# One ring of three tiles for the experts' relu results and the statistics' loads

## The chip, the cores and the metric

The kernel runs on one core of a Trainium2 chip. The metric is the device time of one execution in microseconds (us); the median of several runs is given. A profile of one execution shows what each engine did: TensorE (PE; PEld is its weight load), VectorE (DVE), ScalarE (ACT), GpSimd (POOL) and SyncE (SP), which here issues nearly all DMAs.

## The reference, cut to what matters

Two layers on images of 8 x 384 channels x 32 x 32 in float32. The first is a selective state space scan with a group norm before it and an MLP behind it, the second a mixture of four experts of which each token weighs two.

```python
def reference(x, ...):
    # layer 0: group norm, layer norm, in_proj, conv, silu, scan over 1024 tokens with 16 states,
    #          gate, out_proj, MLP with gelu
    x = x + _L0_conv_ref(_gn(x), ...)
    # layer 1: group norm, gate softmax, top 2, and for each expert e:
    #   hdn = relu(x @ w1[e] + b1[e]);  y = hdn @ w2[e] + b2[e];  out = sum_e coef[e] * y
    x = x + _L1_conv_ref(_gn(x), ...)
    return x
```

The group norm takes a mean and a variance over 12 channels and all tokens of an image. So the statistics of an image must be complete before its first product.

## The kernel before

The 8 images are cut into 16 chunks of 512 tokens (`NCH`), two to an image; a chunk's activations are three tiles of 128 channels x 512 tokens. The scan has 24 rounds for each chunk, 384 in all (`scan_chains`). A round has four exponentials on ScalarE (the decays, line 842), four scans on DVE (line 862), a drive product on POOL (line 854), a read-out on DVE and one on POOL (line 866), and a sum over states on TensorE (line 888). Everything else fills the room beside the rounds: the input projection of the next chunk (`in_proj`, line 328), the output projection of the last one (line 539), the MLP (`hidden`, line 561; `second`, line 603), and the first products of the experts (line 714), which come last in rank.

The order of instructions on all engines is fixed while the program is built. A planner keeps a clock of its own for each engine; costs such as `MM`, `ACT`, `DVE` and `DMA` (3.5 us) are written at the top of the file. Every piece of work is a task, a Python generator that yields the engine it wants next and the time it will take; `yield "-", us` means to wait so long, `yield "bank", us` to wait for one of four PSUM banks as well. `issue_one` picks for each engine a late task, else the next step of a round, else a task that fits. What the planner thinks of time thus decides only the order; on the chip each engine runs through its list and waits on semaphores.

Two kinds of work use the tiles that the change touches.

The statistics of the next image (`statistics`, begun in the third round of an even chunk) read the image once more, in six pieces of 128 x 512 (256 KB). Each piece is loaded by SP into the tile `part` (line 264), and DVE takes its sums (`bn_stats`, line 267). There is one such tile, in the pool `pst`. The first image is read from the tiles of its chunks instead.

The experts' first products come in units (`expert_lane`): 12 for each chunk, 192 in all, each of three products with weights from a stream of three buffers (`e_w`, loaded by SP, line 240). A unit's PSUM bank is emptied by `expert_evict`: ScalarE writes the relu into a tile `r` (line 728), and SP writes that to DRAM (line 731). There are two such tiles, in the pool `pr`. A list `writing` holds the units on their way, and a third one has to wait, with its bank, until one has left the list, 3.5 us of the planner's clock after its write-out was given out. On the chip the relu waits until the write-out of the tile's last content has really landed.

The first half of the units of chunk 13 and all before it can be placed beside the scans; the others come behind them (lines 708 and 709). After the scans `second_layers` reads the relu results back and forms the experts' second products (line 1210), 1152 matmul records in a row.

Of the kernel before, what the change touches and what calls it, by code (L numbers as in the profile page):

```python
# [11 lines left out]
F32 = mybir.dt.float32  # L12
# [6 lines left out]
P = 128  # L19
B, C, L = 8, 384, 1024  # L20
T = 512
# [4 lines left out]
ND = DI // P  # L26
NS = 16
Q = 4
NG = NS // Q
TOP = 16.0  # L30
HID = 9
# [16 lines left out]
POLL = 0.5  # L48
# [9 lines left out]
def chunk_of(dram, i):  # L58

    b, h = divmod(i, NH)  # L60
    return dram[b].rearrange("(p j) (n s) w -> n p j (s w)", p=P, n=NH)[h]
# [6 lines left out]
def build(tc, io):  # L68
# [3 lines left out]
    with ExitStack() as outer:  # L72
# [47 lines left out]
        with ExitStack() as ctx:  # L120
            layers(ctx, tc, io, ident, cmean, eps, dram, x1_dram, gn1, logits, r_dram, group_norm)


def layers(ctx, tc, io, ident, cmean, eps, dram, x1_dram, gn1, logits, r_dram, group_norm):
# [9 lines left out]
    def pool(name, bufs, stack=ctx, **kw):  # L134
        return stack.enter_context(tc.tile_pool(name=name, bufs=bufs, **kw))


    wp, p2, px1, pxn = pool("wp", 1), pool("p2", 2), pool("px1", 2), pool("pxn", 1)
    psq, pr, pw_e = pool("psq", 2), pool("pr", 2), pool("pw_e", 3)
    ps_g = pool("ps_g", BANKS, space=PSUM)  # L140
    scanning = ctx.enter_context(ExitStack())
    p1, pdt, pxt, pdu = (pool(name, bufs, scanning)
                         for name, bufs in (("p1", 1), ("pdt", 2), ("pxt", NH), ("pdu", 3)))
    pz, pxc, ph, pbc, pst = (pool(name, bufs, scanning)
                             for name, bufs in (("pz", ND), ("pxc", 2 * ND), ("ph", HID), ("pbc", NG), ("pst", 1)))
    pw_in, pw_out, pw_1, pw_2 = (pool("pw_" + name, 3, scanning) for name in ("in", "out", "1", "2"))
    ps_a, ps_b, ps_y = (pool("ps_" + name, 1, scanning, space=PSUM) for name in "aby")

# [69 lines left out]
    def bank(name):  # L218
        held[0] += 1
        current[0].holds += 1  # L220
        return ps_g.tile([P, T], F32, name=name, tag="g")

    def free():
        held[0] -= 1
        current[0].holds -= 1
# [26 lines left out]

    def statistics(b):
        st = p2.tile([P, NH * J, 6], F32, name="st")
        for k in range(NH):
            for j in range(J):
                if b == 0:
                    part = xt[k][:, j, :]  # L260
                else:
                    yield "-", 8
                    part = pst.tile([P, T], F32, name="part")
                    nc.sync.dma_start(part, chunk_of(io["x"], b * NH + k)[:, j, :])
                    yield "-", 2 * DMA
                yield "DVE", DVE
                V.bn_stats(st[:, k * J + j, :], part)
        g = wp.tile([P, 2], F32, name=f"gn{b}")
        yield from group_norm(st, bank, free, p2, g)

        yield "bank", 0.25
        small = bank("shift")
        PE.matmul(small[:, 0:1], lhsT=cmean, rhs=g[:, 1:2], start=True, stop=True)
        yield "ACT", 0.65
        mean_w = p1.tile([P, P], F32, name="mean_w")
        S.activation(mean_w, cmean, AF.Identity, scale=g[:, 0:1])
        S.activation(g[:, 1:2], small[:, 0:1], AF.Identity, bias=g[:, 1:2], scale=-float(J))
        yield "-", 0
        free()
        gn[b] = g, mean_w  # L280
# [416 lines left out]
    def expert_lane():  # L697

        for i in range(NCH):
            if i < NCH - NH:  # L700
                yield from load_xn(i)
            while i not in scored:
                yield "-", POLL

            xn = xns.pop(i) if i < NCH - NH else x1[i]
            for u in range(E * J):

                while i == NCH - NH - 1 and u >= E * J // 2 and summed.get(NCH - 1) != J:
                    yield "-", POLL
                yield "bank", 3 * MM  # L710
                w = streams["e_w1"].take("e_w1", u)
                h = bank("e_hid")
                for j in range(J):
                    PE.matmul(h, lhsT=w[:, j, :], rhs=xn[:, j, :], start=(j == 0), stop=(j == J - 1))  # L714

                current[0].holds -= 1
                begin(expert_evict(h, i, u), rank=1, after=now[0] + 3 * MM, holds=1)
            yield "-", 0

    writing = []  # L720

    def expert_evict(h, i, u):
        while len(writing) == 2:
            yield "-", POLL
        writing.append((i, u))
        yield "ACT", ACT
        r = pr.tile([P, T], F32, name="r")
        S.activation(r, h, AF.Relu, bias=e_b1[:, u:u + 1])
        yield "-", 0
        free()  # L730
        nc.sync.dma_start(r_dram[i][u], r)
        yield "-", DMA
        writing.remove((i, u))


    coef_dram = dram.tile([NT, E, P], F32, name="coef_dram")
# [307 lines left out]
    def plan(i, k):  # L1044

        n = i + 1
        if k % 4 == 1 and k // 4 + 2 < ND:
            begin(delta(i, k // 4 + 2), rank=0)
        if k in (2, 3, 4):
            begin(gate(i, k + 1))  # L1050
        if k == 4:
            begin(silus(zs, gates, [(i, d) for d in range(3, 6)]))
        if n < NCH:
            if 4 <= k < 10:
                begin(conv(n, k - 4), rank=1)
            if k in (6, 9):
                begin(silus(xc, accs, [(n, k - 6 + d) for d in range(3)]), rank=1)
            if k in (11, 12, 13):
                begin(gate(n, k - 11))
            if k == 9:  # L1060
                begin(x_proj(n), rank=1)
            if k == 13:
                begin(silus(zs, gates, [(n, d) for d in range(3)]))
            if k == 15:
                begin(delta(n, 0), rank=0)
            if k == 20:
                begin(delta(n, 1), rank=0)
        if k == 20 and n + 1 < NCH:
            begin(norm(n + 1), rank=1)
        if k == 3 and i + NH < NCH:  # L1070
            begin(next_x(i))
        if k == 3 and i % NH == 0 and i + NH < NCH:
            begin(statistics(i // NH + 1), rank=3)
# [169 lines left out]
    with tc.manual_schedule():  # L1243
        w_in = Stream(pw_in, [("in_proj", k) for k in in_order()])

        begin(statistics(0), idle_products())
        run(everything)
        begin(norm(0))
        run(everything)
        S.preload_act_table_set(SILU_SET)  # L1250
        begin(*(conv(0, d, at_once=True) for d in range(ND)), x_proj(0))
        run(lambda: len(xc) == ND)
        exp_ln_tables()
        run(everything)
        load_b(0, 0)
        load_c(0, 0)
        begin(delta(0, 0))
        run(everything)
        for s in range(1, NG):
            load_b(0, s)  # L1260
            load_c(0, s)
        begin(delta(0, 1), rank=0)
        begin(*(gate(0, d) for d in range(3)))
        begin(silus(zs, gates, [(0, d) for d in range(3)]))
        begin(norm(1))
        seed(0, 0)
        begin(lanes())
        scan_chains()
        run(lambda: summed.get(NCH - 1) == J)
        scanning.close()  # L1270
        second_layers()
# [41 lines left out]
```

## Time and profile before

| | |
|---|---|
| median of 3 runs | 3779.09 us (3776.12 to 3780.9) |
| the profiled execution | 3780.1 us |
| its span, first to last instruction | 3778.4 us |
| mean granted TensorE clock | 0.968 |
| busy: PE, DVE, POOL, ACT | 3586.7, 3027.0, 2771.8, 2377.7 us |
| relus of the experts (line 728) | 192 of 682 ns (median), from 700.0 to 3278.9 us |
| loads for the statistics (line 264) | 42, landing after 4.0 us (median), issued from 103.7 to 2500.8 us |
| second products of the experts (line 1210) | from 3278.6 us to the end |

The span has a beginning of some 650 us in which the pipeline fills, the scans with all fillers to about 3103 us, a stage of what is left over, and from 3279 us the second products of the experts. A matmul of float32 shows as two records in the profile. A busy share is a mean over these stages.

### The profile page before, as it was taken

What the parts mean: (1) busy time and instruction counts of PE and PEld (TensorE: products, weight loads), DVE (VectorE), ACT (ScalarE), POOL (GpSimd) and SP (SyncE); (2) the same over time, 40 slices, a digit from 0 to 9 for tenths busy, and PEclk for the clock granted to TensorE, in tenths of its full rate; (3) what the DMA queues carried; (4) which work ended last, traced back from release to release, by engine and by line L of the source; (5) the groups of instructions that cost most, each with busy time, mean ns of one, the idle gap of its engine ahead of it and who ended that gap; (6) DMA issues with size and microseconds to landing.
All of it is one profiled execution on the core that took longest, in us unless ns stands there. A gap on an engine that the chain in (4) does not pass through costs nothing.

```text
span 3778.4 us, 35513 instructions
## 1 busy us (share of the span) xinstructions
PE 3586.7 (95%) x10342; PEld 1369.7 (36%) x10342; DVE 3027.0 (80%) x3099; ACT 2377.7 (63%) x3714; POOL 2771.8 (73%) x1069
## 2 busy tenths in 40 slices
PE   7769898999999999999999999999999999999999
PEld 3213232333333333333333333333333333444444
DVE  4898999899889888998899898988898870355554
ACT  4657686877786778777877787787777753200000
POOL 2998999999889998999889998998899970000000
PEclk8769898999999999999999999999999999999999
DMA  3434454565656565656555555655555543655553
GB/s 118 143 126 148 153 173 160 180 201 184 200 180 203 183 194 181 211 183 202 187 195 191 183 186 175 208 194 181 183 193 191 192 160 131 227 184 184 184 190 105
DMA packets 387925, 674.78 MB, mean 179 GB/s; under 512 B 42876, under 2 KB 153852, under 8 KB 385556
## 3 DMA queue, kind: packets, MB, share of 16 engines
q1 hardware_dynamic: 385568, 672.18, 53.6%
q8 instruction: 83, 1.36, 0.2%
q14 instruction: 110, 0.90, 0.1%
q10 hardware_dynamic: 2164, 0.34, 0.1%
HBM read 534.33 MB, written 138.02 MB: 178 GB/s over the span
## 4 chain that ended last, share of the span: by engine, by line
PE 60%; DVE 13%; ACT 11%; POOL 7%; issue 4%; DMA 4%; SPq 1%; POOLq 0%; DVEq 0%; ACTq 0%
PE acc L1210 13%; PE e_hid L714 9%; PE acc L603 8%; PE hid L561 7%; PE g_in L328 7%; PE y L888 6%; DVE da_A L862 5%; POOL du L854 5%; PE g_out L539 4%; DVE du L862 4%; ACT da_A L842 3%; DVE du L866 2%; POOL du L866 2%; PE g_dt L455 2%; ACT da_B L842 1%
## 5 line engine op out<-in xcount | busy, mean ns | idle before, releaser
L854 POOL TENSOR_TENSOR du<-dxr,b 128x2048 f32<-128x2048 f32 x383 | 1735.1, 4536 | 62.6 <-PE y L888 46.2
L866 POOL TENSOR_TENSOR du<-du,c 128x1024 f32<-128x1024 f32 x384 | 905.8, 2359 | 137.8 <-DVE du L862 107.3
L842 ACT ACTIVATE da_A<-dtr_a,w_a_log 128x512 f32<-128x512 f32 x768 | 529.4, 689 | 262.9 <-DVE du L866 105.8
L842 ACT ACTIVATE da_B<-dtr_b,w_a_log 128x512 f32<-128x512 f32 x768 | 525.9, 685 | 253.4 <-DVE du L862 240.7
L328 PE MATMUL g_in<-xt,in_proj 128*128 128x512 f32 x1152 | 549.7, 619 | 24.4 <-ACT xt L319 11.3
L862 DVE TENSOR_TENSOR_SCAN du<-da_B,carry,du 128x512 f32<-128x512 f32 x384 | 487.7, 1270 | 90.1 <-ACT da_B L842 81.6
L603 PE MATMUL acc<-h,mlp_w 128*128 128x512 f32 x1152 | 538.6, 607 | 12.3 <-ACT h L577 5.3
L888 PE MATMUL y<-du,sel 128*32 128x512 f32 x3072 | 470.4, 629 | 78.0 <-DVE du L866 40.8
L862 DVE TENSOR_TENSOR_SCAN da_A<-da_A,carry,du 128x512 f32<-128x512 f32 x384 | 491.4, 1280 | 53.5 <-ACT da_A L842 49.2
L561 PE MATMUL hid<-tt,mlp_w 128*128 128x512 f32 x1152 | 522.5, 598 | 9.7 <-ACT sq L675 1.8
L862 DVE TENSOR_TENSOR_SCAN du<-da_B,du 128x512 f32<-128x512 f32 x384 | 464.4, 1209 | 68.6 <-ACT da_B L842 46.2
L862 DVE TENSOR_TENSOR_SCAN da_A<-da_A,du 128x512 f32<-128x512 f32 x384 | 467.6, 1218 | 45.3 <-ACT da_A L842 37.2
L1210 PE MATMUL acc<-r,w_e_w 128*128 128x512 f32 x1152 | 494.6, 592 | 0.0
L714 PE MATMUL e_hid<-xn,e_w 128*128 128x512 f32 x1008 | 470.5, 606 | 24.2 <-DMA e_w<-in_e_w 15.0
L866 DVE TENSOR_TENSOR du<-da_A,c 128x1024 f32<-128x1024 f32 x384 | 467.7, 1218 | 9.0
L328 PEld LDWEIGHTS g_in<-xt,in_proj 128*128 128x128 f32 x1152 | 216.6, 195 | 346.8 <-issue 270.2
L603 PEld LDWEIGHTS acc<-h,mlp_w 128*128 128x128 f32 x1152 | 211.0, 191 | 324.9 <-issue 253.7
L561 PEld LDWEIGHTS hid<-tt,mlp_w 128*128 128x128 f32 x1152 | 213.1, 190 | 302.9 <-issue 249.9
L1210 PEld LDWEIGHTS acc<-r,w_e_w 128*128 128x128 f32 x1152 | 218.9, 190 | 275.5 <-issue 275.5
L714 PEld LDWEIGHTS e_hid<-xn,e_w 128*128 128x128 f32 x1008 | 188.6, 192 | 284.0 <-issue 233.1
L539 PE MATMUL g_out<-xc,out_proj 128*128 128x512 f32 x576 | 268.8, 606 | 1.8 <-DMA out_proj<-in_out_proj 1.8
L888 PEld LDWEIGHTS y<-du,sel 128*32 128x32 f32 x3072 | 71.2, 109 | 412.5 <-issue 110.3
(133 smaller groups left out, 3061.8 us busy)
## 6 DMA issues: line engine op xcount, KB each, us to landing
dxr<-dxr_dram SPq DMA_DIRECT2D x384, 256.0 KB, 4.7
mlp_w<-in_mlp_w SPq DMA_DIRECT2D x384, 192.0 KB, 3.6
dtr_b<-dtr_dram SPq DMA_DIRECT2D x192, 256.0 KB, 4.0
dtr_a<-dtr_dram SPq DMA_DIRECT2D x192, 256.0 KB, 3.2
r_dram<-r SPq DMA_DIRECT2D x192, 256.0 KB, 3.3
r<-r_dram SPq DMA_DIRECT2D x64, 768.0 KB, 4.6
in_proj<-in_in_proj SPq DMA_DIRECT2D x192, 192.0 KB, 3.4
e_w<-in_e_w SPq DMA_DIRECT2D x192, 192.0 KB, 3.9
```

What stands on the lines that cost most here:

```text
L328: PE.matmul(g, lhsT=w[:, j, :], rhs=xt[i][:, j, :], start=(j == 0), stop=(j == J - 1))
L455: PE.matmul(g, lhsT=w_dt[:, d * P:(d + 1) * P], rhs=dbc[i][0:DTR, :], start=True, stop=True)
L539: PE.matmul(g, lhsT=w[:, d, :], rhs=xc[i, 3 * k + d], start=(k + d == 0), stop=(k == 1 and d == 2))
L561: PE.matmul(g, lhsT=w[:, j, :], rhs=tt[i][:, j, :], start=(j == 0), stop=(j == J - 1))
L603: PE.matmul(g, lhsT=w[:, n, :], rhs=hs[mine[n]], start=(k + n == 0), stop=(k == 1 and n == 2))
L714: PE.matmul(h, lhsT=w[:, j, :], rhs=xn[:, j, :], start=(j == 0), stop=(j == J - 1))
L842: S.activation(out, dtr[i, d][pair][:, j % 2, :], AF.Exp, scale=neg_a[:, d, j, s:s + 1])
L854: G.tensor_tensor(du[r], dxr[i, d], wide(bt[i, s].unsqueeze(1), [P, Q, T]), ALU.mult)
L862: V.tensor_tensor_scan(a if j < 2 else b, a, b, start, ALU.mult, ALU.add)
L866: engine.tensor_tensor(du[r][:, js, :], h, wide(ct[i, s].unsqueeze(1), [P, 2, T]), ALU.mult)
L888: PE.matmul(y[j * m:(j + 1) * m, :], lhsT=sel, rhs=h[:, j, :], start=False, stop=(s == NG - 1), tile_position=(0, j * m), skip_group_check ...
L1210: PE.matmul(acc[j], lhsT=e2[:, e, d, j, :], rhs=r[:, d, :], start=(e + d == 0), stop=(e + d == E + J - 2))
```

## The change

The pool `pst` and the list `writing` go. The pool `pr` gives out three tiles once, `r0` to `r2`, and a list `spare` holds those that are free. A task that needs one takes the first of the list, or asks again each 0.5 us of the planner's clock, and appends it at the end of the list when it is done: the experts 3.5 us after the write-out was given out, the statistics as soon as `bn_stats` has been given out. The experts take their tile before they ask for ScalarE, the statistics theirs before the load. So up to three relu results can be on their way while no statistics are loaded, and the room in memory is the same.

```diff
-    psq, pr, pw_e = pool("psq", 2), pool("pr", 2), pool("pw_e", 3)
+    psq, pr, pw_e = pool("psq", 2), pool("pr", 1), pool("pw_e", 3)
...
-    pz, pxc, ph, pbc, pst = (pool(name, bufs, scanning)
-                             for name, bufs in (("pz", ND), ("pxc", 2 * ND), ("ph", HID), ("pbc", NG), ("pst", 1)))
+    pz, pxc, ph, pbc = (pool(name, bufs, scanning)
+                             for name, bufs in (("pz", ND), ("pxc", 2 * ND), ("ph", HID), ("pbc", NG)))
...
+    spare = deque(pr.tile([P, T], F32, name=f"r{k}") for k in range(3))
+
     def statistics(b):
...
                     yield "-", 8
-                    part = pst.tile([P, T], F32, name="part")
+                    while not spare:
+                        yield "-", POLL
+                    part = spare.popleft()
                     nc.sync.dma_start(part, chunk_of(io["x"], b * NH + k)[:, j, :])
                     yield "-", 2 * DMA
                 yield "DVE", DVE
                 V.bn_stats(st[:, k * J + j, :], part)
+                if b > 0:
+                    spare.append(part)
...
-    writing = []
-
     def expert_evict(h, i, u):
-        while len(writing) == 2:
-            yield "-", POLL
-        writing.append((i, u))
+        while not spare:
+            yield "-", POLL
+        r = spare.popleft()
         yield "ACT", ACT
-        r = pr.tile([P, T], F32, name="r")
         S.activation(r, h, AF.Relu, bias=e_b1[:, u:u + 1])
         yield "-", 0
         free()
         nc.sync.dma_start(r_dram[i][u], r)
         yield "-", DMA
-        writing.remove((i, u))
+        spare.append(r)
```

## The prediction

> **What bounds the kernel now.** I read the page's busy shares first, then the busy time by stretches, then the TensorE gaps in the timeline, and last the answer for the tile r, since the change is about when that tile comes free.
>
> ```profile
> PE 3586.7 (95%) x10342; PEld 1369.7 (36%) x10342; DVE 3027.0 (80%) x3099; ACT 2377.7 (63%) x3714; POOL 2771.8 (73%) x1069
> ```
>
> TensorE is busy 95% of the span. The missing 192 us are not spread evenly. The stretches (columns: stretch, length, busy of PE, PEld, DVE, ACT, POOL, clock, DMA share, GB/s):
>
> ```profile
> 189.00:283.00 94.00, 60.92 (x156) 14.75 (x156) 85.70 (x89) 53.18 (x85) 91.04 (x40) 0.66 0.37 126
> 1134.00:1512.00 378.00, 369.28 (x1125) 137.42 (x1123) 339.06 (x341) 292.67 (x457) 347.75 (x133) 0.99 0.58 191
> 1889.00:2267.00 378.00, 366.10 (x1120) 137.34 (x1118) 342.14 (x345) 290.93 (x458) 343.85 (x132) 0.99 0.58 189
> 2645.00:3023.00 378.00, 372.51 (x1143) 139.41 (x1140) 332.34 (x329) 289.22 (x437) 352.07 (x135) 1.00 0.57 190
> 3306.00:3400.00 94.00, 94.00 (x220) 41.61 (x219) 50.07 (x57) 0.00 (x0) 0.00 (x0) 1.00 0.52 184
> ```
>
> Most idle time is in the first 650 us, where POOL is the fuller engine and no expert product exists yet. From 650 us to the last scan (3103 us) TensorE idles only 51 us, adding up its gaps in the timeline, and POOL and DVE run at 89 to 93%. After 3279 us it never stops. A change in the experts' relu tiles can win at most a part of those 51 us, and a few in the stage between 3103 and 3279 us. The tile r:
>
> ```profile
> L728 ACT ACTIVATE r<-e_hid,w_e_b x192: 665/682/694, 700.0 to 3278.9; 128x512 f32<-128x512 f32 x192
>   DMA r_dram<-r: 44.7, 19
> DMA to landing us min/median/max: 2.0/4.3/12.0
> ```
>
> In 19 of 192 cases ScalarE, which works in order, stood before a relu until an earlier write-out of the same tile had landed, 44.7 us together. Six of these (17.0 us) come after 3160 us. The other thirteen (27.7 us) stand in the scans, where decays (line 842) queue behind the relu. One shows the whole damage:
>
> ```profile
> 2145.49 0.69 ACT L728 ACTIVATE r<-e_hid,w_e_b 128x512 f32<-128x512 f32 x1 [3.17 <-DMA r_dram<-r]
> 2146.08 0.68 ACT L842 ACTIVATE da_B<-dtr_b,w_a_log 128x512 f32<-128x512 f32 x1
> ...
> 2147.55 0.38 PE L273 MATMUL shift<-gn,cmean 128*128 128x1 f32 x2 [4.21 <-ACT gn L116]
> ...
> 2149.12 5.49 PE L290 MATMUL mu<-xt,mean_w 128*128 128x512 f32 x6 [1.18 <-ACT mean_w L276]
> ```
>
> The relu waits 3.17 us, the statistics chain behind it is late, TensorE stands 4.21 us, and then six matmuls take 5.49 us in place of 2.74: the clock granted in 2148 to 2156 us is 0.56 to 0.58. The gap itself and the slow matmuls (2.75 us) and sums (1.36 for 1.06) after it are all paid.
>
> **Is TensorE really the bound?** The Trainium skill, Perfetto Trace Analysis, section Identifying the Most-Contended Engine, holds matmul busy time a bad measure and wants the weight loads' share, here 36%. By that rule TensorE has room, gaps on it are free, and the sum below would lose its only positive term: 3775. The trace speaks otherwise: twelve expert units near the end, 72 matmul records back to back, take 31.14 us, 0.43 us each, and nothing else limits them. Float32 products fill TensorE although weights load quickly. I take the row, and charge gaps.
>
> **The change part by part.**
>
> *The same work.* No instruction is added or removed: still 192 relus, 192 write-outs, 42 loads for statistics, 42 bn_stats. Three 128x512 tiles before (two r, one part), three after. What changes is who may have which, and, as the order of all engines is written down by the planner while the program is built, the order. In the changed program TensorE's order is the same up to the 2100th of 5174 instructions (about round 189 of 384, near 1600 us). From there 138 of the 384 rounds stand with a different count of expert products, mostly one or two units ahead, and at the last round both have given out 161 units. The 31 units left over after the scans, and TensorE's and DVE's order from there, are the same.
>
> *Waits on the write-out.* A write-out frees its tile 0.68 + 4.3 = 5.0 us after the relu starts. With two tiles that is one relu per 2.5 us, and a unit takes TensorE 31.14/12 = 2.6 us, so two tiles just carry the median; every late landing (up to 12.0) makes a wait. Here the skill speaks against the change: DMA: Bandwidth & Descriptors, section Anatomy of one DMA, fits 2.0 us fixed plus bytes over 436 GB/s, an estimate of 2.6 us for 256 KB, so (0.68 + 2.6)/2 = 1.6 us per relu. By that rule two tiles were plenty and the third is worth nothing; by the row it is worth the waits. I take the row, as the waits are there. In the changed order no relu of the scans finds its tile written by one of the last 7 ScalarE instructions (before: 10 relus did), and within 10 instructions 3 do (before: 27). So nearly all of the 27.7 us goes from ScalarE. What TensorE gets of it: I take each gap that follows such a wait, at most as long as the wait: 1.24 (1390 us, where the expert's weights landed late in the same moment, so it may stay), 3.17 (2147), 0.59 (2898), 0.74 (2929): 5.7 us, and 3.05 for the slow clock after 2147, 8.8 at most. The other waits, some 22 us, have no TensorE gap near them: cover is TensorE's own queue, which holds some microseconds of ready products; without it they would be won too. Only the 1.24 lies in the part whose order stays; in place of the rest another gap may come. Value: -5, most of the 6.2 at 2147; ends 0 and -8.8.
>
> *Statistics in the ring.* A load holds a tile for the planner's 7 us and the wait for DVE, 36 times while experts run: then the experts have two tiles, as before. A load now also waits, on the SP queue, for the last write-out of its tile. In three cases the two stand only 4, 6 and 7 SP instructions apart; at 0.3 to 0.5 us an issue, the landing of 4.3 us leaves 2.5, 1.5 and 1 us of waiting, with weight loads and the dtr and dxr repeats queued behind. SP stands idle for 250 us for relus alone (its own waits), and what it issues is wanted microseconds later, so I take 0; without that cover 5 us. No relu got a wait on DVE, though a tile is given back when bn_stats is issued: ScalarE has always waited for a later DVE instruction already: 0. The statistics themselves have 17 + 24 rounds of 8 us before they are needed, against six loads of some 20 us: 0.
>
> *The new order from round 189.* Per round POOL needs 4.54 + 2.36 + 1.27/4 = 7.2 us, so a stretch of rounds with less than 7.2 us of TensorE work each leaves it dry, unless it is behind. I put TensorE's work on the rounds (0.86 per 128x512 product, 1.06 per round's sums). Over 8-round stretches, rounds 176 to 384, the shortfall comes to 19.2 us before and 24.6 after; over 4 rounds 40.2 and 44.0; over 3 rounds 57.0 and 58.0. The 8-round figure is near the 25 us that TensorE really idled from 1650 us on, so I weigh it about half: +3; ends 0 and +7. The trace can't show gaps of an order that hasn't run: a newly drawn order of that length could as well have 15 or 40 us of gaps for these 25.
>
> *After the scans.* TensorE stands 2.72 us for h, 6.00 and 1.40 us for e_w. The first e_w is queued on SP behind the stores of x1, the last behind the coefficients, as in the new order. ScalarE's 17.0 us there hold up nobody. In the new order three e_w loads stand behind the write-out of the unit that frees their buffer, 0.77 us later than now: 0 to +2.3, value 0. From 3279 us: 0.
>
> Sum: the profiled execution took 3780.1 us (span 3778.4 and 1.7 around it), 1.0 above the median of 3779.1. 3780.1 - 5 + 3 = 3778.1.
>
> **The rivals.** *Nearly nothing (likeliest), 3778.* The waits go, most are covered, and the order gives back part. For it: the 51 us of gaps in 2450 us, the same tail.
>
> *Faster, 3768.* All 8.8 us come back, the weak stretches cost nothing because TensorE is behind there, and the redrawn part loses a few more gaps of e_w and xn: 3780.1 - 8.8 - 3. For it: a gap of 9 us in all waits for e_w since 650 us. Against: those stand mostly where no relu waited.
>
> *Slower, 3796.* Experts let go earlier leave later rounds without filling. In the new order rounds 213 to 220 are 9.0 us short (before 1.2) and 357 to 364 are 8.4 (before 6.6): 9.6 us more, and if each comes as one stand of over 3 or 4 us, the slow clock adds 3.05 twice: 3780.1 + 9.6 + 6.1 = 3795.8, with no wait won. It decides once the shortfall is larger than the products TensorE still has queued. Against: shortfalls of 6.5 us before (rounds 305 and 357) left no gap over 3 us.
>
> *It doesn't do what it says.* If clumps of four relus came as often as clumps of three, the third tile would change nothing: 3780 with any order. The distances on ScalarE speak against it.
>
> **How the numbers follow.** Likeliest case 0.51, faster 0.22, slower 0.27. About 0.2%, 7.6 us, is what a measurement of this kernel can tell from no change: below 3771.5 counts as faster, above 3786.7 as slower; the likeliest case lies between, with its own range 3772 to 3786. The unknown is the gaps of the new order, 15 to 40 for 25 us, and clock losses after them, so the range goes from 3762 to 3797.
>
> **What would show it.** Waits of r on r_dram before 3103 us should fall from 27.7 us to under 8. TensorE's gaps before 1600 us should be about 1 us fewer. From 1600 to 3103 us they should stay within 15 to 40 us; the places to look are rounds 213 to 220 (about 1760 to 1830 us) and 357 to 364 (2910 to 2970). The stage from 3103 us should keep its length of 675 us within 2. I am wrong if gaps over 3.5 us with a clock of 0.5 after them appear, or if POOL starts to wait for dxr behind a statistics load on SP.

## The result, and the profile after

The changed kernel takes 3792.11 us (median of 9 runs, 3784.2 to 3796.11) where the kernel before takes 3779.09 (9 runs): 1.0029 of it, 95% interval 1.0021 to 1.0038. It is slower by 11 us, 8 to 14. The likeliest forecast was no change.

The page of the changed kernel shows nearly the same sums:

```profile
PE 3584.2 (95%) x10342; PEld 1369.9 (36%) x10342; DVE 3028.1 (80%) x3099; ACT 2379.6 (63%) x3714; POOL 2771.1 (73%) x1069
```

The span is 9.9 us longer, and TensorE is busy 2.5 us less, so some 12 us more of gaps. The stretches (the same columns as before: PE, PEld, DVE, ACT, POOL, clock, DMA share, GB/s):

```profile
1134.00:1512.00 378.00, 370.16 (x1125) 138.61 (x1124) 342.15 (x345) 293.85 (x459) 348.64 (x134) 0.99 0.58 190
1889.00:2267.00 378.00, 364.75 (x1119) 136.56 (x1117) 335.57 (x338) 286.90 (x452) 339.30 (x131) 0.99 0.57 191
2645.00:3023.00 378.00, 373.95 (x1152) 139.67 (x1145) 334.13 (x329) 294.85 (x444) 352.07 (x134) 0.99 0.57 189
3306.00:3400.00 94.00, 94.00 (x220) 41.61 (x219) 52.05 (x59) 0.00 (x0) 0.00 (x0) 1.00 0.55 190
```

From 1889 to 2267 us all engines do less in the same time than before (POOL 339.3 us for 343.9, DVE 335.6 for 342.1). The last stage is unchanged. The tile r answers as follows; the change's own effect is complete:

```profile
L731 ACT ACTIVATE r<-e_hid,w_e_b x192: 664/681/690, 701.5 to 3288.4; 128x512 f32<-128x512 f32 x192
...
L268 SPq DMA_DIRECT2D r<-in_x x42: 327/430/592, 104.6 to 2501.9; - x42
...
  PE e_hid L720: 138.5, 70
```

There is no line for r_dram left. 44.7 us of waits on the write-out are gone. Instead the relus wait for TensorE, 138.5 us in 70 cases where it was 83.8 in 43. This alone is no sign of a loss: a relu that no longer waits for its tile waits for its product instead, and a faster kernel below shows 107.2 us in 51 cases. The loss shows where TensorE stands before its expert products (line 720, 714 before). One such place in the timeline (start, length, engine, instruction, in brackets the idle time before it):

```profile
1982.91 1.07 PE L891 MATMUL y<-du,sel 128*32 128x512 f32 x8
...
1983.53 2.43 SPq L380 DMA_DIRECT2D xn<-xn_dram  x3
...
1989.32 4.58 PE L720 MATMUL e_hid<-xn,e_w 128*128 128x512 f32 x6 [5.34 <-ACT da_B L845]
...
1993.74 2.74 PE L545 MATMUL g_out<-xc,out_proj 128*128 128x512 f32 x6
...
1993.94 0.69 ACT L731 ACTIVATE r<-e_hid,w_e_b 128x512 f32<-128x512 f32 x1 [5.28 <-PE e_hid L720]
```

Between 1982.9 and 1989.3 TensorE has just finished the last unit of a chunk, and its next instruction is the first unit of the next chunk. Both use the one tile xn, so the three pieces of the new chunk can be loaded only now, from 1983.53 on, and a piece lands 5.0 us after its issue (median). The profile names a decay as the releaser, but that decay is no input of this product; I take the loads to have landed last, which the runs without them test below. Then the six matmuls run at half clock at first, 4.58 us in place of 2.74. I call this a switch.

### The profile page after: what moved, and what is told of

Same layout as the page of the kernel before. It is cut to its first block, busy times and chain, and to the rows that moved or that the text cites. A ratio compares the mean times of both kernels' runs of the same rounds, so it can differ in the third digit from the quotient of the medians.

```text
span 3788.3 us, 35527 instructions
## 1 busy us (share of the span) xinstructions
PE 3584.2 (95%) x10342; PEld 1369.9 (36%) x10342; DVE 3028.1 (80%) x3099; ACT 2379.6 (63%) x3714; POOL 2771.1 (73%) x1069
## 4 chain that ended last, share of the span: by engine, by line
PE 62%; DVE 14%; ACT 13%; POOL 4%; DMA 4%; issue 3%; SPq 1%; DVEq 0%; POOLq 0%; ACTq 0%
PE acc L1213 13%; PE e_hid L720 9%; PE acc L609 9%; PE hid L567 8%; PE g_in L334 8%; PE y L891 6%; DVE da_A L865 6%; PE g_out L545 5%; DVE du L865 4%; ACT da_A L845 3%; POOL du L857 2%; DVE du L869 2%; PE g_dt L461 2%; ACT L208 2%; ACT da_B L845 2%
## 5 line engine op out<-in xcount | busy, mean ns | idle before, releaser
L334 PE MATMUL g_in<-xt,in_proj 128*128 128x512 f32 x1152 | 547.3, 616 | 23.9 <-DMA in_proj<-in_in_proj 10.2
```

What stands on the lines that cost most here:

```text
L334: PE.matmul(g, lhsT=w[:, j, :], rhs=xt[i][:, j, :], start=(j == 0), stop=(j == J - 1))
```

## The experiments

Theory A: the cost lies in the new order, at the experts' own loads, above all at switches of xn that have nothing between. Theory B is, in the first run, that sharing the ring costs the time on SP and ScalarE, and later that any newly drawn order is worse in many small places. Ratios are to the kernel before on the same chip; 0.1% is 3.8 us. "The same order" means that all instructions of an engine stand in the same sequence.

**The ring without the third result.** The changed kernel with at most two results on their way. Its engines all have the order of the kernel before.

```diff
+    writing = []
+
     def expert_evict(h, i, u):
-        while not spare:
+        while not spare or len(writing) == 2:
             yield "-", POLL
         r = spare.popleft()
+        writing.append(u)
...
         spare.append(r)
+        writing.remove(u)
```

> The changed kernel's ring of three tiles, shared with the statistics, but with at most two expert results on their way as before. All five engines then have exactly the order of the kernel before. Theory A (the cost is the new order that a third result on its way gives, by chunk switches on the single tile xn): 3772 to 3780 us, since only the waits of relus on write-outs go away, and no wait of r on r_dram is left before 3100 us. Theory B (the cost is in the sharing itself: loads on the SP queue behind write-outs, relus behind bn_stats): about 3790 us, like the changed kernel, with new waits at those two lines.

3772.88 us, 0.9971 (0.9960 to 0.9982): faster than both kernels. Theory B in its first form is out: with the order of before, the shared ring gains 7 to 15 us. Its answers for the tile r and TensorE:

```profile
  DMA r_dram<-r: 1.3, 1
```
```profile
2145.70 0.38 PE L279 MATMUL shift<-gn,cmean 128*128 128x1 f32 x2 [0.99 <-ACT gn L116]
2147.82 5.49 PE L296 MATMUL mu<-xt,mean_w 128*128 128x512 f32 x6 [1.74 <-ACT mean_w L282]
```

One wait on a write-out is left, and at the place of the prediction's example TensorE's two gaps fall from 4.21 and 1.18 us to 0.99 and 1.74. At the chunk switch that the changed kernel has tight, its TensorE reads:

```profile
1977.08 2.84 PE L720 MATMUL e_hid<-xn,e_w 128*128 128x512 f32 x6
1979.76 5.31 PE L545 MATMUL g_out<-xc,out_proj 128*128 128x512 f32 x12
1985.01 1.12 PE L461 MATMUL g_dt<-dbc,w_dt_proj 24*128 24x512 f32 x2
1986.06 1.07 PE L895 MATMUL y<-du,sel 128*32 128x512 f32 x8
1987.05 2.84 PE L545 MATMUL g_out<-xc,out_proj 128*128 128x512 f32 x6
```

After the unit of line 720 it goes on with the output projection, and no new chunk is wanted. So the whole loss comes with the new order, which only the third result on its way makes: 1.0029 against 0.9971, 0.58% (0.44 to 0.72%), 22 us. The profiles agree: from the read-out of round 192 to the end the changed kernel takes 2182.5 us (2185.6 in a second profile), the ring in the old order 2167.3, and TensorE's gaps from 1600 us to the last scan add up to 34.73 us (37.62) against 21.95. Most of the loss is gaps.

**Leaving out the reloads of xn.** In both orders, xn is kept from the first chunk.

```diff
-    xns, xn_dram = {}, {}
+    xns, xn_dram, kept = {}, {}, {}
...
-        xn = pxn.tile([P, J, T], F32, name="xn")
-        yield from in_pieces(xn, xn_dram[i], False)
+        xn = kept.setdefault("xn", None) or pxn.tile([P, J, T], F32, name="xn")
+        if kept["xn"] is None:
+            kept["xn"] = xn
+            yield from in_pieces(xn, xn_dram[i], False)
+        else:
+            for j in range(J):
+                yield "-", 0
         yield "-", DMA
```

> The changed kernel in its own order, but the tile xn is loaded only for the first chunk and kept: the 39 later loads of 256 KB are left out, so the experts compute on the first chunk's input. Theory A (the switches of xn cost the time): the TensorE gaps at the switches near 833, 1226, 1605 and 1989 us go, with the half clock after them; 3789 minus some 25 us, 3760 to 3770, and level with the kernel before with the same loads left out within 5 us. Theory B (the new order is worse in many small places, as any newly drawn order): both lose about the same few us, and the 12 us between the two stay.

> The kernel before in its own order with the same 39 loads of xn left out. Theory A: its two tight switches (831 and 1222 us) go, 2.0 + 5.1 us of gaps and 2.6 us of slow clock after the second: about 3768 us. Theory B: the same; what counts is the distance to the changed kernel with xn kept, under 5 us by A, about 12 us by B.

3774.5 us, 0.9976 (0.9967 to 0.9985), and 3773.92 us, 0.9970 (0.9958 to 0.9982). They are level, as theory A said; of the some 25 us that it gave the changed kernel without these loads, 20 came. But this comparison alone proves less than it seems: the first has the ring and the second has two tiles and 44.2 us of waits on write-outs, so the ring's gain hides in it. The fair partner is the ring in the old order:

> The ring with at most two results on their way (order of the kernel before), and the 39 later loads of xn left out, so that the experts compute on the first chunk's input. It splits the 20 us between the two orders: with the ring alike in both, this one stands against after_xn_kept (0.9976 of the kernel before). If the switches of xn are the whole cost of the new order, both are level within 3 us (about 3774 where the kernel before takes 3785). If the ring's gain of 0.29% and the switches' gain of 0.30% add up, it is near 0.994 (3763) and some 12 us of the new order's cost have another source than xn, such as expert units in a row whose weights come late.

3763.8 us, 0.9957 (0.9943 to 0.9971). Without xn loads the new order still costs 0.19% (0.02 to 0.36%), 7 us.

**More room at the switch.** The planner is told of 3 x 3.5 us for a load of xn, for the changed kernel and for the ring with two results.

```diff
         yield from in_pieces(xn, xn_dram[i], False)
-        yield "-", DMA
+        yield "-", 3 * DMA
```

> The changed kernel with the planner told that a load of xn takes 3 x 3.5 us in place of 3.5, so it puts other products between the last unit of a chunk and the first of the next (at least 13 us of TensorE work in place of 1 to 4 us at five switches). Nothing else is changed, but the order is drawn anew from the first switch on. Theory A: no gap of e_hid on xn or right behind its load; 3765 to 3778 us. Theory B: a new order like any other, 3785 to 3800 us.

> Ring of three, at most two results on their way, and the planner told that a load of xn takes 3 x 3.5 us. If what is won by tiles and what is won at the switches add up: 0.994 to 0.995 of the kernel before, better than each alone (0.997). If the switches' gain is used up by a newly drawn order: 0.997.

3772.6 us, 0.9966 (0.9953 to 0.9979), and 3769.2 us, 0.9971 (0.9960 to 0.9982). The first turns the changed kernel from slower to faster, with three results on their way and no wait for xn among its larger ones. It is a new order throughout, though, so it supports the switches as the cause and does not prove it. On top of the ring with two results the same edit gains nothing.

**The changed kernel once more.**

> The changed kernel itself once more, on the same chip as its rivals and for a second profile: 1.003 of the kernel before. If the gaps at the xn switches (near 833, 1226, 1605, 1989 us) and near 2146 us with the half clock after them are of the order, they stand there again within 1 us; if they are chance of one execution, they don't.

3789.91 us, 1.0027 (1.0018 to 1.0036). The gaps stand again at the same instructions: 5.83 us at 1222, 2.53 at 1601, 5.73 at 1987, 3.86 at 2144. The clock at the third (busy PE, records, clock, DMA share, GB/s):

```profile
1983.00:1987.00 4.00, 0.49 (x1) 0.76 1.05 397
1987.00:1991.00 4.00, 4.00 (x6) 0.50 0.72 266
```

The slow matmuls near 833 us that the first profile had (5.46 us for six) were chance: they took 2.81 us this time.

**The two new switches alone.** The order leaves 3.6 and 1.1 us of TensorE work (0.86 us a product) for the switches to chunks 5 and 7, where the kernel before has 35.5 and 39.1. (A third one near 3083 us, with gaps of 1.3 and 2.0 us in the two profiles, is left as it is.) In the changed order the loads of xn for these two chunks are left out, and in a control those for chunks 4 and 6.

```diff
-    xns, xn_dram = {}, {}
+    xns, xn_dram, kept = {}, {}, {}
...
-        xn = pxn.tile([P, J, T], F32, name="xn")
-        yield from in_pieces(xn, xn_dram[i], False)
+        if i not in (5, 7):          # (4, 6) in the control
+            xn = kept["xn"] = pxn.tile([P, J, T], F32, name="xn")
+            yield from in_pieces(xn, xn_dram[i], False)
+        else:
+            xn = kept["xn"]
+            for j in range(J):
+                yield "-", 0
```

> The changed kernel in its own order, with xn left unloaded for chunks 5 and 7 alone (6 of 42 loads; these two compute on the input of chunks 4 and 6). Their switches have 3.6 and 1.1 us of TensorE work between the last unit of the chunk before and the first of their own, where the kernel before has 35.5 and 39.1. If these two switches carry most of the new order's cost, the time falls from 1.0028 of the kernel before by 10 to 14 us, to 0.9990 to 1.0002, and the gaps near 1602 and 1987 us with the half clock after them are gone. If the cost is spread over the order, it falls by no more than in after_without_xn_4_6.

> The same with chunks 4 and 6, whose switches have 99 us of TensorE work between in both orders, so that as many loads are left out where nobody waits: 1.002 to 1.003 of the kernel before, no different from the changed kernel.

1.0015 (1.0006 to 1.0023) against 1.0032 (1.0021 to 1.0043) for the control: 0.17% (0.03 to 0.31%), 6 us, and not the 10 to 14 expected. TensorE without the loads, and in the control:

```profile
1982.71 1.07 PE L896 MATMUL y<-du,sel 128*32 128x512 f32 x8
1983.70 2.84 PE L725 MATMUL e_hid<-xn,e_w 128*128 128x512 f32 x6
1986.38 2.74 PE L545 MATMUL g_out<-xc,out_proj 128*128 128x512 f32 x6
```
```profile
1981.69 1.07 PE L896 MATMUL y<-du,sel 128*32 128x512 f32 x8
1987.91 5.46 PE L725 MATMUL e_hid<-xn,e_w 128*128 128x512 f32 x6 [5.15 <-DMA xn<-xn_dram]
```

Here the profile names the load itself. 5.15 us of gap and 2.7 of slow clock go at this place, but not all of it is kept. By the starts of the rounds' read-outs on DVE, in one profile each, the kernel without the loads is 1.0 us behind the control at round 240, 4.5 us ahead at round 248 and 3.6 ahead at the last round. The switch to chunk 5 brings 1.4 us by round 200, lost again by round 216. So the two switches are worth less than their gaps.

**Leaving out the expert weights too, and alone.** A second new gap is no switch: TensorE meets four expert units nearly in a row, and the third one's weights are late, since a weight buffer is free only when the unit three before has been multiplied, and the load is queued on SP behind others. In the second profile of the changed kernel, and on POOL in the first:

```profile
2144.40 7.61 PE L720 MATMUL e_hid<-xn,e_w 128*128 128x512 f32 x12 [3.86 <-DMA e_w<-in_e_w]
```
```profile
2157.26 4.53 POOL L857 TENSOR_TENSOR du<-dxr,b 128x2048 f32<-128x2048 f32 x1 [4.33 <-DMA b<-bc_dram]
```

The load of b stands on SP behind a weight load and a write-out that wait for the slow unit, and so POOL stands as well.

```diff
-            self.ahead = pool.bufs - 1
+            self.ahead, self.first = pool.bufs - 1, {}
...
+                if name == "e_w1" and self.loaded >= 3:
+                    self.tiles[self.loaded] = self.first[self.loaded % 3]
+                    self.loaded += 1
+                    return
                 t = self.tiles[self.loaded] = self.pool.tile([P, 3, P], F32, name=name, tag="w")
+                self.first[self.loaded % 3] = t
                 nc.sync.dma_start(t, io[name][k])
```

> The changed kernel in its own order, with xn kept from the first chunk and, besides, the expert weights kept from the first three units: 39 loads of xn and 189 of e_w are left out, so the experts' results are those of other inputs. With xn kept alone the new order still cost 0.19% (0.9976 against 0.9957, some 7 us). If that rest is units in a row whose weights come late (2146 us, 3.9 us and the half clock after it) and what SP holds back behind those weights (POOL's wait of 4.3 to 4.8 us for b), this kernel is level with ring_cap2_no_expert_loads within 3 us. If it is spread over the whole new order, in the shortfalls of TensorE work, some 7 us stay.

> The ring with at most two results on their way, so the order of the kernel before, with the same loads of xn and e_w left out. Below 0.9957 of the kernel before, as e_w waits (9 us of gaps since 650 us and 6 us behind the scans) go too: 0.992 to 0.994. It is the yardstick for after_no_expert_loads.

> The changed kernel in its own order with the expert weights kept from the first three units (189 loads of e_w left out), xn loaded as in the changed kernel. Together with ring_cap2_no_e_w it fills the table of the two orders with and without the loads of xn and of e_w: the new order costs 0.57% with both, 0.19% without xn, 0.14% without either. If the 10 us that are still open lie in late e_w (2146 us and the like), the cost without e_w is near 0.3%. If they lie in the switches of xn besides those of chunks 5 and 7, or in what xn and SP hold up, it stays at 0.5%.

> The ring with at most two results on their way (order of the kernel before), 189 loads of e_w left out, xn loaded: 0.9971 less some 10 us of e_w gaps, 0.993 to 0.995. It is the yardstick for after_no_e_w.

Measured: 0.9924 (0.9911 to 0.9936) and 0.9910 (0.9895 to 0.9926) without either load; 0.9966 (0.9954 to 0.9978) and 0.9932 (0.9918 to 0.9946) without e_w alone. The table is complete; each cost is the difference of the two ratios, with an uncertainty of some 0.15 to 0.2% (6 to 8 us):

| loads left out | ring, new order | ring, old order | cost of the new order |
|---|---|---|---|
| none | 1.0029 | 0.9971 | 0.58%, 22 us |
| xn | 0.9976 | 0.9957 | 0.19%, 7 us |
| e_w | 0.9966 | 0.9932 | 0.34%, 13 us |
| xn and e_w | 0.9924 | 0.9910 | 0.14%, 5 us |

Both orders leave out the same loads, so what less traffic alone brings is alike in both. Some 17 of the 22 us hang on the experts' own loads. The split is not sharp, since the two interact: leaving out xn saves 15 us of the cost, or 8 once e_w is out; leaving out e_w saves 9, or 2 once xn is out. The last 5 us are no more than their uncertainty, but the profiles of the two kernels without either load point the same way: TensorE's gaps from 1600 us to the last scan are 22.0 us in the new order and 15.2 in the old.

**An order drawn anew with two tiles.** The kernel before, with only the planner's time of a write-out changed:

```diff
-        yield "-", DMA
+        yield "-", 1.2 * DMA
         writing.remove((i, u))
```

> The kernel before with its two tiles and its own tile for the statistics; only the planner's time of a write-out is 4.2 us in place of 3.5, which draws the order anew. Its switches of xn have 3.6, 3.6 and 3.6 us of TensorE work at three early places and 3.6 at the last (before: 3.6 and 1.1, and 6.2). By the theory of the switches it is slower by one more tight switch, 5 to 10 us (1.0013 to 1.0026); if any new order costs some 0.3 to 0.5%, 1.003 to 1.005; if the cost hangs on three results on their way, level with the kernel before.

3798.65 us, 1.0049 (1.0036 to 1.0061): worse than the changed kernel, without a third tile, a third result or sharing, and more than the one further tight switch was to cost. Its waits on write-outs are those of before, and its products of experts wait for their loads too:

```profile
  DMA r_dram<-r: 45.3, 16
```
```profile
1784.75 4.51 PE L714 MATMUL e_hid<-xn,e_w 128*128 128x512 f32 x6 [4.62 <-DMA e_w<-in_e_w]
```

So the loss isn't special to three results. The size is what was put on record for "any new order", yet new orders are not worse as such: the two with more room at the switch were at 0.9966 and 0.9971. What an order costs here seems to hang on how the planner pictures these loads: it holds e_hid ready 3.5 us after the last piece of xn is given out, and does not ask whether e_w has landed at all. For the kernel with two tiles this is argued from its gaps; no run left its loads out.

## Why the prediction was wrong

- *TensorE as the bound.* Right: gaps were paid for. Against the ring in the old order the new one had 12.8 and 15.7 us more of them in the two profiles and took 15.2 and 18.3 us longer from round 192 on. By the weight loads' share alone they would have been free. The section cited for that share names a second measure beside it, the share of the peak rate of operations, which the prediction left out. (A reading that changes nothing: DVE's lowest stretch shown from 650 us on is 88%, not 89.)
- *Waits on the write-out.* Right in kind, too small in size. They fell from 44.7 us to none (under 8 before 3103 us was said), and with the old order that is worth 0.29% (0.18 to 0.40%), 7 to 15 us, where -5 (at most -8.8) was taken. One part was mis-reasoned: in the ring with the old order the 3.05 us of slow clock at 2147 us stayed with the smaller gaps (5.49 us for six matmuls again). Which of the waits held for covered were paid after all is not shown.
- *Two tiles were plenty, by the skill's fixed cost of a DMA.* The trace was rightly preferred: the third tile was worth 7 to 15 us. The section cited gives its fit for DMAs that GpSimd issues, and SyncE issues these, so its 2.6 us was no estimate for them; they landed after 4.3 us (median).
- *Statistics in the ring.* Right: 0. The loads of line 268 waited 1.5 us in all for write-outs, and no relu waited for DVE.
- *The new order from round 189.* This step failed: +3 us, ends 0 and +7, against 22 us. With the two terms as measured the sum is 3780.1 - 11 + 22 = 3791. The step counted how much TensorE work each round has, and not what a product needs besides TensorE. The numbers that gave it away were there: the changed order has given out 60 units by round 192 where the old one has 59, and 84 by round 240 for 83. 60 and 84 are multiples of 12: at just these rounds one unit more ends a chunk and brings the reload of xn into the next instruction. The work per round, which the step did measure, may be the 5 us that stay without any expert load, within its range; 2.36 us of them can be pointed at (see the rival "slower").
- *After the scans.* Right: that stage and the last one together are about 1 us longer.
- *The rival "slower".* It gave 3796, mainly by the wrong mechanism. In its first stretch (rounds 213 to 220) TensorE stood 3.6 us, 2.8 of it for a weight load of the MLP, and in its second no longer than before (2.35 us for 2.69). But there the cause has changed. Before, TensorE stood for an expert's weights; in the new order it stands for the round's own read-out, which is what scarce work looks like, and it still does with no expert load left (2.36 us):

```profile
2929.28 4.51 PE L714 MATMUL e_hid<-xn,e_w 128*128 128x512 f32 x6 [2.69 <-DMA e_w<-in_e_w]
```
```profile
2940.66 1.06 PE L891 MATMUL y<-du,sel 128*32 128x512 f32 x8 [2.35 <-DVE du L869]
```

So the rival's mechanism exists, at a few us; the larger new gaps lie where a load is late. That 3796 is near the 3792 measured is luck.
- *Signs to look for.* TensorE's gaps from 1600 us to the last scan were 34.7 and 37.6 us in the two profiles (27.1 before), inside the 15 to 40 given, so that this test was too weak; from 650 to 1600 us they did not shrink (24.6 and 23.7 for 23.9). The sign named for being wrong did come: new gaps of 5.3 and 3.9 us, at 1989 and 2146 us, with a clock of 0.50 and 0.51 in the 3 us after them. POOL did wait behind SP, for b and not for dxr.

## What to carry to other kernels

When a planner writes the order down, judge a change of its limits by the order that it yields, and look in that order for single-buffered tiles: how much work lies between the last use of the old content and the first use of the new, against the landing time of its load. A limit that looks like a mere throttle (two results on their way) can be what keeps a low-ranked lane from running into its own loads. In this kernel that was luck of one order and no property of the limit: with the same two tiles, the same limit and another planned time for a write-out the kernel was slower still (1.0049). Take the resource and the limit apart in an experiment: the three tiles with the old limit beat both kernels (0.9971).

## What the runs showed of the hardware

The length of a gap alone did not tell whether TensorE's clock would drop after it. At the same instruction near 830 us, a gap of 3.04 us left six matmuls at 2.81 us (the ring with two results), and one of 2.80 us made them take 5.46 (the changed kernel, first profile). In the ring with two results the gaps of 0.99 and 1.74 us, with 0.38 us of matmuls between them, were enough: the granted clock from 2147.5 to 2153.3 us was 0.50. The Trainium skill, TensorE: Matmul & The Clock Gate, section Part 1, lets the clock fall after an idle window of some 3.4 us that runs free of the kernel; the free-running window fits the chance seen here, the full idle window does not, as these gaps were shorter. Gaps of 5 us and more at the switches were followed by half clock in every profile here: the next six matmuls took 4.6 to 5.5 us in place of 2.74.
